# Gated cross-attention and mixture of experts: five more expert blocks with the weights as the stationary operand, and row scatters tied to VectorE's products

## The chip, the cores and the metric

The kernel runs on one core of one Trainium2 chip. The metric is device time in microseconds (us) of the whole program, the median of repeated executions of one compiled program. A separate execution was profiled; every duration quoted below comes from it.

## The reference, cut to what matters

32 sequences of 128 tokens with 128 features go through a cross-attention layer (16 heads, added through a tanh gate) and then through a layer of experts. The change lies in the expert layer alone:

```
h = layernorm(x)                                  # 4096 tokens x 128
scores = sigmoid(h @ gate_w.T)                    # 32 experts in 4 groups of 8
# the 2 best groups, in them the 8 best experts; weights normalised, times 2.5
final[t] = sum over the chosen e of w[t,e] * down_e( silu(h gate_e) * (h up_e) )
x = x + tanh(g_ffn) * (final + shared_mlp(h))
```

All data are float32. Every token uses the 16 experts of exactly two groups, those not chosen with weight zero. So a token is sorted by its pair of groups (six pairs), and a block is 128 tokens of one pair, which need two group halves of 8 experts with 64 hidden units each.

## The kernel before, in words

The program first does attention, 32 sequences one after another (up to about 300 us), then a stretch in which the last sequences, the shared expert and the sorting overlap (to about 334 us), then a loop over expert blocks, number j = 0 to 34, which the profile shows from 334 us to about 536 us. Two more blocks stand behind a branch at the end.

**Sorting in three batches.** `choose(k)` is a generator that does the expert choice and computes a row number for each token. It is advanced in small pieces by `gap(room, transfers)`, placed by hand into the instruction order; after its pieces `gap` issues up to `transfers` waiting scatters through `put_rows`. One scatter is `put(i)`, L698: GpSimd (POOL) writes 128 token rows (16 weights, 128 features, the token's number; 145 floats) to their sorted places in the DRAM table `xs`. The batches have 12, 8 and 12 scatters. Batch 2 serves the last stage, blocks 15 to 36; batch 1 serves blocks 7 to 14 and batch 0 blocks 0 to 6. `SHARE` is (7, 8, 22), `NBLK` is 37 and `NSURE` is 35.

**Loading.** `load(j)`, L1100, reads a block's 128 sorted rows into `xb` on the queue of SyncE (SP), in 16 buffers. The first load of a batch waits for all its scatters to land. `more_loads(must, may)` issues loads up to block `must` in any case, and up to `may` once the scatters of that batch have all been issued.

**Two forms of a block.** In a narrow block `xprep` turns the tokens on TensorE (PE, L1116), `gate_up` makes two products of 512 columns, the tokens being the stationary operand (L1124, L1126), VectorE (DVE) multiplies by weights (`uw`, L1131) and by the SiLU (`h`, L1136), and `turned_hidden` turns the hidden values on PE (L1144) and copies them out on ScalarE (ACT, L1146). In a wide block the expert weights are stationary: `gate_up_wide` makes 16 matmuls of 128 columns per half (L1190), the hidden values come out turned already, and no `turned_hidden` is needed. In exchange ACT copies the group's weights to a fixed place (`place_weights`, L1182, two copies per half), and the routing weights must stand as 128 equal rows: `turn_weights` transposes them on PE (L1158, L1159) and sends 8 KB to DRAM (`wr`, L1165, on SP), and `spread_weights` reads that back into `wb` with two broadcast transfers of 256 KB (L1170, on SP). DVE then uses `wb` (L1196) and makes `h` (L1198). Both forms end in `down` (L1206) and `finish`: ACT scales the result (`o`, L1215) and POOL adds it to the output rows with an indirect DMA (L1217).

**The order in the loop.** It is written out by hand. Iteration j issues the two halves of block j + 1's gate and up products, with block j's `down` between them, `xprep` or `place_weights` for j + 2, and at its end `turn_weights` and `spread_weights` for block j + 3 if that is wide. A block's token number column is read by DVE in `number` (L1112), which waits for the load. All engines run their own instructions in order. The products g and u have two PSUM buffers each.

```
    def wide(j):
        return j >= NBLK - SHARE[2] + 2      # 17 and above
```

Of the kernel before, what the change touches and what calls it, by code (L numbers as in the profile page):

```python
# [12 lines left out]
ALU = mybir.AluOpType  # L13
# [24 lines left out]
NBLK = B + NC - 1  # L38
TAIL = (NC - 1) * P
NSURE = NBLK - 2  # L40
# [8 lines left out]
SHARE = (FULL[0], FULL[1] - FULL[0], NBLK - FULL[1])  # L49
# [5 lines left out]
def gated_cross_attention_moe(  # L55
# [236 lines left out]
    v = nc.vector  # L292
# [213 lines left out]

    filled = {-1: base}
    sorts = []
    tab = const.tile([1, NBLK, 4], I32, tag="tab", name="tab")
    ready = [False] * 3  # L510

    def choose(k):
# [5 lines left out]
        def small(name, *shape):  # L518
            return r1.tile([P, *shape], F32, tag=name, name=f"{name}_{k}")


        other = nc.gpsimd if k == 0 else v
# [74 lines left out]
        at = 0  # L597
        for g in range(NG - 1):
            w = NG - 1 - g
# [79 lines left out]
        row = small("row", n, NC)  # L679
# [17 lines left out]
        def put(i):  # L697
            w = nc.gpsimd.indirect_dma_start(  # L698
                out=xs[:, :], out_offset=bass.IndirectOffsetOnAxis(ap=posi[:, i : i + 1], axis=0),
                in_=rows[:, first[k] + i, :], in_offset=None, bounds_check=NROWS - 1,  # L700
            )

            if sorts:
                tc.declare_no_dep(w.ins, group="sorts", reason="no two tokens have one row")
            tc.add_to_no_dep_group("sorts", w.ins)
            sorts.append(w.ins.name)
# [83 lines left out]
    def step_on(value=None):  # L790
        try:
            piece[:] = [batches[0].send(value)]
        except StopIteration:
            batches.popleft()
            piece.clear()

    def put_rows(n):
        for _ in range(min(n, len(pending))):
            _, put, i = pending.popleft()
            put(i)  # L800

    def gap(room, transfers=1):

        fresh = True
        while batches and 3 - len(batches) < opened:
            if not piece:
                step_on()
                continue
            w = piece[0]
            if w == "n":  # L810
                if not fresh:
                    break
                step_on()
            elif w in ("pe", "act"):
                break
            else:
                if room <= 0:
                    break
                room -= w
                step_on()  # L820
            fresh = False
        put_rows(transfers)
# [259 lines left out]
    xbs, wrows, wbs, wcs, own, xTs, groups, hs, hTs, ys, idx = ({} for _ in range(11))  # L1082

    def stage(j):
        return max(i for i in range(3) if sum(SHARE[:i]) <= j)
# [35 lines left out]
    def gate_up(j, s):  # L1121
        at = groups[j][s] * FG
        g = ps_g.tile([P, FG], F32, tag="g", name=f"g_{j}_{s}")
        nc.tensor.matmul(g, xTs[j], eg_all[:, bass.ds(at, FG)], start=True, stop=True)  # L1124
        u = ps_g.tile([P, FG], F32, tag="u", name=f"u_{j}_{s}")
        nc.tensor.matmul(u, xTs[j], eu_all[:, bass.ds(at, FG)], start=True, stop=True)  # L1126
        a = m3.tile([P, FG], F32, tag="act", name=f"act_{j}_{s}")
        nc.scalar.activation(a, g, AF.Silu)
        uw = m3.tile([P, FG], F32, tag="uw", name=f"uw_{j}_{s}")
        w = xbs[j][:, 0:NEP].rearrange("p (t s q) -> p s q t", t=2, s=2)[:, s]  # L1130
        v.tensor_tensor(  # L1131
            uw.rearrange("p (q t f) -> p q t f", t=2, f=64), u.rearrange("p (q t f) -> p q t f", t=2, f=64),
            w.unsqueeze(3).to_broadcast([P, GE // 2, 2, 64]), ALU.mult,
        )
        h = m4.tile([P, FG], F32, tag="h", name=f"h_{j}_{s}")
        v.tensor_tensor(h, a, uw, ALU.mult)  # L1136
        hs[j, s] = h

    def turned_hidden(j, s):
        h = hs.pop((j, s))  # L1140
        n = FG // P
        pt = small_psum(f"ph_{j}_{s}").rearrange("p (q n) -> p q n", n=P)
        for q in range(n):
            nc.tensor.transpose(pt[:, q, :], h[:, q * P : (q + 1) * P], ident)  # L1144
        hT = m3.tile([P, n, P], F32, tag=f"hT{s}", name=f"hT_{j}_{s}")
        nc.scalar.copy(hT, pt)  # L1146
        hTs[j, s] = hT
# [3 lines left out]


    def wide(j):
        return j >= NBLK - SHARE[2] + 2

    def turn_weights(j):
        pt = small_psum(f"px_{j}").rearrange("p (k n) -> p k n", n=P)
# [26 lines left out]
    def gate_up_wide(j, s):  # L1184
        n = FG // P
        g, u = (ps_g.tile([P, n, P], F32, tag=k, name=f"{k}_{j}_{s}") for k in "gu")
        w = wcs.pop((j, s))
        for k, pt in enumerate((g, u)):
            for q in range(n):
                nc.tensor.matmul(  # L1190
                    pt[:, q, :], w[:, k, q * P : (q + 1) * P], xTs[j], start=True, stop=True
                )
        a = m3.tile([P, n, P], F32, tag="act", name=f"act_{j}_{s}")
        nc.scalar.activation(a, g, AF.Silu)
        uw = m3.tile([P, n, P], F32, tag="uw", name=f"uw_{j}_{s}")
        v.tensor_tensor(uw, u, wbs[j][:, s], ALU.mult)  # L1196
        hTs[j, s] = m4.tile([P, n, P], F32, tag="h", name=f"h_{j}_{s}")
        v.tensor_tensor(hTs[j, s], a, uw, ALU.mult)  # L1198

    def down(j, s):  # L1200
        hT = hTs.pop((j, s))
# [35 lines left out]
    AHEAD = 3  # L1237
# [5 lines left out]
    def more_loads(must, may):  # L1243
        while loaded_[0] < NSURE and (
            loaded_[0] <= must or (loaded_[0] <= may and complete(stage(loaded_[0])))
        ):
            load(loaded_[0])
            loaded_[0] += 1

    with tc.manual_schedule():  # L1250
        more_loads(AHEAD, AHEAD)
        hsh = {}

        def up(t):
            g = ps_g.tile([P, TT], F32, tag="g", name=f"sg_{t}")
            u = ps_g.tile([P, TT], F32, tag="u", name=f"su_{t}")
            up_products(t, g, u)
            a = m3.tile([P, TT], F32, tag="act", name=f"sa_{t}")
            hsh[t] = m4.tile([P, TT], F32, tag="h", name=f"sh_{t}")
            gated(g, u, a, hsh[t])  # L1260

        def down_base(t):
            y = ps_y.tile([P, TB, D], F32, tag="y", name=f"sy_{t}")
            down_products(y, hsh.pop(t))
            base_out(t, y, m4.tile([P, TB, D], F32, tag="so", name=f"so_{t}"))

        up(4)
        up(5)
        gap(1.2, 2)
        down_base(4)  # L1270
        psum_place("prs_4")
        gap(1.2, 2)
        up(6)
        pt = small_psum("pt2")
        turn2(pt, 28, 4)
        turned2_out(pt, 28, 4)
        down_base(5)
        gap(1.2, 2)
        pl = small_psum("pl2")[:, 0 : 8 * E]
        logits(pl, 24, 8)  # L1280
        logits_out(pl, 24, 8)
        psum_place("prs_5")
        logits_done(24, 8)
        up(7)
        gap(1.2, 2)
        xprep(0)
        down_base(6)
        psum_place("prs_6")
        gap(1.2, 2)
        opened = 3  # L1290
        gate_up(0, 0)
        xprep(1)
        down_base(7)
        gate_up(0, 1)
        for j in range(AHEAD + 1):
            number(j)
        turned_hidden(0, 0)
        done = -1
        for j in range(NSURE):
            more = j + 1 < NSURE  # L1300
            more_loads(j + AHEAD, j + 13)
            if more:
                (gate_up_wide if wide(j + 1) else gate_up)(j + 1, 0)
            if j + 2 < NSURE and wide(j + 2):
                place_weights(j + 2, 0)
            if done < j - 1:
                finish(j - 1)
                if j - 1 + AHEAD < NSURE:
                    number(j - 1 + AHEAD)
            down(j, 0)  # L1310
            if not wide(j):
                turned_hidden(j, 1)
            if j + 2 < NSURE and not wide(j + 2):
                xprep(j + 2)
            psum_place(f"prb_{j}")
            gap(1.4, 2)
            if more:
                (gate_up_wide if wide(j + 1) else gate_up)(j + 1, 1)
            if j + 2 < NSURE and wide(j + 2):
                place_weights(j + 2, 1)  # L1320
            down(j, 1)
            if not wide(j) or not more:
                finish(j)
                done = j
                if AHEAD < j + AHEAD < NSURE:
                    number(j + AHEAD)
            if more and not wide(j + 1):
                turned_hidden(j + 1, 0)
            if j + AHEAD < NSURE and wide(j + AHEAD):
                turn_weights(j + AHEAD)  # L1330
                spread_weights(j + AHEAD)
            gap(1.4, 1)

# [68 lines left out]
```

## Time and profile before

| what | value |
|---|---|
| median of 3 runs | 548.38 us (547.67 to 548.81) |
| profiled execution, its own time | 551.0 us |
| its span in the profile | 549.2 us |
| granted TensorE clock in it | 0.984 of full |
| PE / DVE / ACT / POOL busy | 94% / 74% / 68% / 50% |
| expert blocks: narrow, wide | 17, 18 |
| scatters of rows (L698) | 32, mean 1.08 us on POOL |
| additions to the output (L1217) | 35, mean 1.58 us on POOL |

The profiled execution's time is 1.8 us above its span, which is what lies around the span, and 2.6 us above the median of the runs. "PE" is TensorE's matmuls and "PEld" its weight loads, which overlap them. In a row of the timeline the columns are start, duration, engine, line, operation, what is written and read, how often, and in brackets the idle time before it with what ended it. "SPq" is the SP queue: such a row is the issue of a transfer and not its duration.

### The profile page before, as it was taken

Reading aid. Unit: us, or ns where it says so; the run is one execution under the profiler, and the core shown is the slowest. Engines: PE = TensorE matmul, PEld = TensorE weight load, DVE = VectorE, ACT = ScalarE, POOL = GpSimd, SP = SyncE. Lnnn points to the kernel's source line nnn. Section 1 sums busy time; section 2 is a strip of 40 time slices with the busy share of each in tenths; the row PEclk is TensorE's granted clock in tenths of the full one; section 3 lists DMA queues with packets and bytes.
Section 4 is the critical chain, followed back from the end, with each engine's and each line's share of the span. In section 5 each row is a group of like instructions: output and inputs, shape, how many; then the busy total and the mean of one; then the engine's idle time right before and its main releaser. Section 6 shows DMA issues by size and latency. Waiting matters only on the chain.

```text
span 549.2 us, 15741 instructions
## 1 busy us (share of the span) xinstructions
PE 514.8 (94%) x5857; PEld 440.9 (80%) x5857; DVE 406.1 (74%) x920; ACT 374.5 (68%) x1407; POOL 276.8 (50%) x248
## 2 busy tenths in 40 slices
PE   5889999999999999998999789999999999999992
PEld 4777888988989988897876556666676799999992
DVE  3779999898898998998887588898644445555551
ACT  1688989989899888997883144444444677777760
POOL 5255557665675756874754641652672212232332
PEclk9899999999999999999999989999999999999997
DMA  8994440805304010000000232131123255453631
GB/s 237 236 331 144 129 174 3 300 4 175 127 20 152 3 42 1 2 2 3 2 2 26 77 94 63 35 72 15 38 49 82 56 118 122 95 131 89 128 88 15
DMA packets 49563, 47.81 MB, mean 87 GB/s; under 512 B 20752, under 2 KB 38848, under 8 KB 49104
## 3 DMA queue, kind: packets, MB, share of 16 engines
q1 hardware_dynamic: 43008, 41.71, 26.6%
q0 software_dynamic: 6192, 4.56, 5.7%
q8 instruction: 48, 0.79, 0.6%
q10 hardware_dynamic: 288, 0.52, 0.4%
q14 instruction: 27, 0.22, 0.2%
HBM read 25.44 MB, written 21.54 MB: 86 GB/s over the span
## 4 chain that ended last, share of the span: by engine, by line
PE 71%; DVE 20%; POOL 2%; ACT 2%; issue 1%; DMA 1%; another core or an unknown queue 1%; POOLq 0%; DVEq 0%
PE y L1206 11%; PE o_ps L436 8%; PE s_ps L369 8%; PE o_ps L415 7%; PE u L1190 6%; PE g L1190 6%; PE o_ps L328 6%; PE g L1124 6%; PE u L1126 5%; DVE nmax L376 5%; DVE eT L404 5%; PE ph L1144 3%; DVE xn L307 3%; DVE oT L424 1%; ACT e L389 1%
## 5 line engine op out<-in xcount | busy, mean ns | idle before, releaser
L389 ACT ACTIVATE e<-s_ps,nmax 128x128 f32<-128x128 f32 x512 | 181.6, 384 | 9.7 <-DVE nmax L376 8.3
L398 POOL TENSOR_TENSOR e<-e,rs 128x1024 f32<-128x1024 f32 x64 | 121.4, 1898 | 92.6 <-DVE rs L396 92.6
L1217 POOL DMA_INDIRECT out_dram<-o,idx x35 | 55.1, 1575 | 128.0 <-ACT o L1215 74.9
L389 ACT ACTIVATION_READ_ACCUMULATOR e<-s_ps,nmax 128x1 f32 x512 | 114.0, 223 | 0.0
L376 DVE TENSOR_REDUCE nmax<-s_ps 128x8 f32<-128x1024 f32 x64 | 77.0, 1202 | 11.7 <-PE s_ps L369 11.5
L404 DVE STREAM_TRANSPOSE eT<-e 128x1024 f32<-128x1024 f32 x64 | 78.7, 1229 | 0.9 <-POOL e L398 0.9
L369 PE MATMUL s_ps<-kvT_sb,qT 64*128 64x128 f32 x1024 | 76.0, 289 | 3.0 <-ACT e L389 1.9
L369 PEld LDWEIGHTS s_ps<-kvT_sb,qT 64*128 64x128 f32 x1024 | 63.7, 191 | 18.7 <-issue 11.1
L436 PE MATMUL o_ps<-c_sb,oT 128*128 128x128 f32 x512 | 65.4, 281 | 6.8 <-DVE oT L424 6.8
L436 PEld LDWEIGHTS o_ps<-c_sb,oT 128*128 128x128 f32 x512 | 59.7, 191 | 13.4 <-DVE oT L424 10.5
L415 PE MATMUL o_ps<-eT,kv 32*64 32x256 f32 x2048 | 66.0, 380 | 2.1 <-DVE c_sb L285 1.0
L328 PE MATMUL o_ps<-xnT,a_sb 128*128 128x128 f32 x480 | 59.9, 278 | 0.0
L1196 DVE TENSOR_TENSOR uw<-u,wb 128x512 f32<-128x512 f32 x36 | 24.9, 692 | 46.4 <-PE u L1190 41.5
L328 PEld LDWEIGHTS o_ps<-xnT,a_sb 128*128 128x128 f32 x480 | 56.7, 194 | 0.3 <-issue 0.2
L415 PEld LDWEIGHTS o_ps<-eT,kv 32*64 32x64 f32 x2048 | 49.4, 131 | 8.1 <-DVE c_sb L285 1.4
L1206 PEld LDWEIGHTS y<-ed_sb,hT 128*128 128x128 f32 x272 | 35.5, 191 | 16.0 <-issue 14.3
L698 POOL DMA_INDIRECT xs<-rows,posi x32 | 34.5, 1078 | 19.7 <-DVE nbi L727 11.0
L1131 DVE TENSOR_TENSOR uw<-u,xb 128x512 f32<-128x512 f32 x34 | 23.3, 686 | 24.2 <-PE u L1126 22.5
L1146 ACT COPY hT<-ph 128x512 f32<-128x512 f32 x34 | 19.9, 586 | 27.1 <-PE ph L1144 20.0
L1190 PE MATMUL g<-xT,wc 128*128 128x128 f32 x288 | 38.0, 275 | 0.0
L1190 PE MATMUL u<-xT,wc 128*128 128x128 f32 x288 | 38.0, 275 | 0.0
L1206 PE MATMUL y<-ed_sb,h 128*128 x288 | 37.8, 275 | 0.0
(203 smaller groups left out, 891.2 us busy)
## 6 DMA issues: line engine op xcount, KB each, us to landing
xs<-zero SPq DMA_DIRECT2D x8, 1740.0 KB, 12.2
wb<-wr SPq DMA_DIRECT2D x36, 256.0 KB, 4.0
kv<-in_kv_dram SPq DMA_DIRECT2D x32, 128.0 KB, 3.1
xb<-xs SPq DMA_DIRECT2D x35, 72.5 KB, 2.2
x_all<-in_x_dram SPq DMA_DIRECT2D x8, 256.0 KB
kvT_sb<-in_kvT_dram SPq DMA_DIRECT2D x6, 256.0 KB, 5.5
eg_sb<-in_exp_gT_dram SPq DMA_DIRECT2D x1, 1024.0 KB, 6.2
eu_sb<-in_exp_uT_dram SPq DMA_DIRECT2D x1, 1024.0 KB
```

What stands on the lines that cost most here:

```text
L328: nc.tensor.matmul(o_ps[1][:, p // HP, p % HP * P : (p % HP + 1) * P], a_sb[:, p].rearrange("d j k -> d (j k)"), x_, start=True, stop=True,)
L369: nc.tensor.matmul(s_ps[g][:, j, q, :], qT[b][r, g * HP + q, :], kvT_sb[r, b * P : (b + 1) * P], start=True, stop=True,)
L376: v.tensor_reduce(nmax[b, g], s_ps[g].rearrange("p j q k -> p (j q) k"), AX.X, ALU.max, negate=True)
L389: nc.scalar.activation(es[b][:, g, j, q, :], s_ps[g][:, j, q, :], AF.Exp, bias=n[:, c], accum_out=sums[b, g][:, c],)
L398: nc.gpsimd.tensor_tensor(e, e, rs.unsqueeze(2).to_broadcast([P, NP, P]), ALU.mult)
L404: v.transpose(eTs[b][:, g].rearrange("p j q n -> p (j q n)"), es[b][:, g].rearrange("p j q n -> p (j q n)"))
L415: nc.tensor.matmul(o_ps[a // 2][j * KV : (j + 1) * KV, a % 2, 0 : NP * Q].rearrange("k (g q n) -> k g q n", g=2, q=HP), kv_sb[b // TB][r, ...
L436: nc.tensor.matmul(o_ps[0][:, 0, 0:D], o[:, p].rearrange("k a n -> k (a n)"), c_sb[:, p, :], start=(p == 0), stop=(p == NP - 1),)
L698: w = nc.gpsimd.indirect_dma_start(out=xs[:, :], out_offset=bass.IndirectOffsetOnAxis(ap=posi[:, i : i + 1], axis=0), in_=rows[:, first[k] ...
L1190: nc.tensor.matmul(pt[:, q, :], w[:, k, q * P : (q + 1) * P], xTs[j], start=True, stop=True)
L1206: nc.tensor.matmul(ys[j], hT[:, q, :], ed_all[:, bass.ds(groups[j][s] * FG + q * D, D)], start=(s == 0 and q == 0), stop=(s == 1 and q == ...
L1217: w = nc.gpsimd.indirect_dma_start(out=out_rows, out_offset=bass.IndirectOffsetOnAxis(ap=idx.pop(j), axis=0), in_=o, in_offset=None, bound ...
```

## The change

`wide` becomes true for blocks 10 to 14 as well, so the narrow blocks are 0 to 9, 15 and 16, and the wide ones 10 to 14 and 17 to 34. Each `h` product that DVE makes is noted in `pace`, and every scatter issued after the first such product waits for the latest one issued before it. The scatters that a `gap` issues change from two in the middle and one at the end of an iteration to one in the middle and two at the end. `more_loads` asks for block j + 2 in place of j + 3 where block j + 3 is narrow.

```diff
@@ choose
+    pace = []
...
             w = nc.gpsimd.indirect_dma_start(
                 out=xs[:, :], out_offset=bass.IndirectOffsetOnAxis(ap=posi[:, i : i + 1], axis=0),
                 in_=rows[:, first[k] + i, :], in_offset=None, bounds_check=NROWS - 1,
             )
+            if pace:
+                tc.add_manual_dep(
+                    w.ins, pace[-1],
+                    mybir.DependencyInfo(mybir.DependencyClass.Sync, mybir.DependencyReason.DATA),
+                    reason="not all at once: transfers in a row hold the other engines up",
+                )
@@ gate_up
-        v.tensor_tensor(h, a, uw, ALU.mult)
+        w = v.tensor_tensor(h, a, uw, ALU.mult)
         hs[j, s] = h
+        pace.append(w.ins.name)
@@ wide
-        return j >= NBLK - SHARE[2] + 2
+        at = j - (NBLK - SHARE[2])
+        return -5 <= at < 0 or at >= 2
@@ gate_up_wide
-        v.tensor_tensor(hTs[j, s], a, uw, ALU.mult)
+        w = v.tensor_tensor(hTs[j, s], a, uw, ALU.mult)
+        pace.append(w.ins.name)
@@ the loop over blocks
-            more_loads(j + AHEAD, j + 13)
+            more_loads(j + AHEAD if j + AHEAD < NSURE and wide(j + AHEAD) else j + 2, j + 13)
...
             psum_place(f"prb_{j}")
-            gap(1.4, 2)
+            gap(1.4, 1)
...
-            gap(1.4, 1)
+            gap(1.4, 2)
```

## The prediction

> **What bounds the kernel now.** I read the page's busy shares and slices first, then PE's timeline in the block loop, then stretches of it with their granted clock, then the timelines of POOL and SP where batch 2 is scattered and loaded.
>
> ```profile
> PE 514.8 (94%) x5857; PEld 440.9 (80%) x5857; DVE 406.1 (74%) x920; ACT 374.5 (68%) x1407; POOL 276.8 (50%) x248
> ...
> PE   5889999999999999998999789999999999999992
> ...
> wb<-wr SPq DMA_DIRECT2D x36, 256.0 KB, 4.0
> ...
> wr<-wq SPq DMA_DIRECT2D x18, 8.0 KB, 1.4
> ```
>
> PE is full from slice 25 to the last but one, so a PE instruction saved in the block loop is time saved, and any wait of PE is time lost. Two iterations, one narrow and one wide, and two idle stretches ahead of the loop (columns: stretch, sum of busy time, PE busy, granted clock, DMA share, GB/s):
>
> ```profile
> 399.57:405.77 6.20, 6.20 (x35) 1.00 0.23 46
> 443.13:448.71 5.58, 5.58 (x53) 1.00 0.56 118
> ...
> 310.00:313.40 3.40, 1.36 (x4) 1.00 0.08 22
> 313.40:316.80 3.40, 3.40 (x5) 0.50 0.34 96
> ...
> 323.60:327.00 3.40, 1.69 (x5) 1.00 0.24 55
> 327.00:330.40 3.40, 3.40 (x11) 0.51 0.67 187
> ```
>
> A narrow block costs PE 6.20 us, a wide one 5.58. After a stretch in which PE was busy for 1.36 or 1.69 of 3.4 us, the clock is halved for the next 3.4 us. Idle times of 0.6 us in the loop did not do that. Now the rows that decide block 14:
>
> ```profile
> 394.98 1.16 PE L1206 MATMUL y<-ed_sb,hT 128*128 x8 [0.32 <-ACT hT L1146]
> ...
> 400.49 1.56 POOL L1217 DMA_INDIRECT out_dram<-o,idx  x1 [0.30 <-issue]
> ...
> 408.62 1.45 POOL L698 DMA_INDIRECT xs<-rows,posi  x1 [0.30 <-issue]
> ...
> 411.69 12.23 SPq L1100 DMA_DIRECT2D xb<-xs  x13
> ...
> 425.24 1.02 PE L1126 MATMUL u<-eu_sb,xT 128*128 x2
> ...
> 431.54 0.34 SPq L1165 DMA_DIRECT2D wr<-wq  x1
> 432.92 1.11 SPq L1170 DMA_DIRECT2D wb<-wr  x2
> ```
>
> The last scatter of batch 2 leaves POOL at 410.07; SP issues the first load of the last stage 1.6 us later, and then 13 in a row at 0.94 us each. A block's `wr` and `wb` go over the same queue, in order.
>
> **The change part by part.**
>
> *PE work of five blocks.* Removed per block: two groups of four transposes (L1144), 0.436 us each. Added: one more token transpose, 0.11, and 16 short matmuls in place of 4 long ones, 0.895 against 0.860 us for each of four products. That is -0.87 + 0.11 + 0.14 = -0.62 us, which is 6.20 less 5.58. Five blocks: **-3.1 us**.
>
> *The hold at 394 us.* Iteration 9 takes 6.79 us instead of 6.20: ACT gets `y` and `ph` late, amid three scatters in a row, and `down` waits for `hT`. With block 10 wide, `down(9, 0)` comes 0.2 us later after the start, and `turned_hidden(10, 0)` is gone. **-0.6 us.** If the hold returns this is 0.
>
> *ACT.* In iteration 8 it has two SiLU (0.60), two hT copies (0.59), four weight copies (0.615), `o` (0.37) and the two copies of `turn_weights` (0.25): 5.7 of 6.3 us. Each hT copy ends before its `down` by my count (the tighter one at 393.7 for 394.9). Cost 0, covered by that 1.2 us; without the cover it delays PE by the excess, at most about 0.6 us.
>
> *The new waits on POOL.* A scatter waits for an `h` product that DVE makes in its own half iteration; queued behind it on POOL are later scatters and `finish`, and behind the last scatter the loads on SP. In batch 2 POOL is behind DVE anyway: after `finish(9)` it has five scatters at 1.30 us apart, and the awaited h(11, 1) is ready at 405.2, when POOL reaches its scatter at 405.5. So the waits bind hardly at all, and groups of three in a row remain. Batch 1: its last scatter now stands behind `finish(3)` and starts at about 362.8 instead of 361.1, so the load of block 7 lands at 367.5 instead of 365.8. DVE's `number(7)` is at its turn at 367.42, and DVE is full there: h(7, 0) ends 0.2 us before PE needs it. **+0.1 us**, between 0 and 0.8.
>
> *SP, and block 14.* This is the large one. Blocks 10 to 13 send their `wr` and `wb` while SP has nothing else, and their weights land 6.9 us after the transposes, as block 17's do now (430.58 to 437.5), ahead of use. Block 14's are issued at the end of iteration 11. But at the start of iteration 11 batch 2's scatters are all issued, and `may` (j + 13 = 24) lets ten loads, blocks 15 to 24, go onto SP ahead of them. In step:
> - Iteration 7 starts at 379.09 as now. Iterations 7 to 13 then last 7.70 (7.48 now, and the two transposes of `turn_weights`, 0.22), 6.31 (6.20 less `xprep`'s 0.11, and 0.22), 6.02 (four products at 0.895, two `down` at 0.89, one group of transposes, 0.22), 5.58, 5.58 (the wide form), 5.37 (no `turn_weights`) and 5.48 us (`xprep` of block 15 again); iteration 14 starts at 421.13.
> - `o(9)` is ready at 399.47, `finish(9)` runs from 399.7 to 401.3, the five scatters follow, the last from 406.8 if each takes 1.0 us. Five of the 20 scatters in the loop take 1.4 to 1.5 now, so I put its end at 408.4 and the load of block 15 at 410.0.
> - Ten loads: the tenth 8.43 us after the first (411.69 to 420.12 now). Then `wr` +0.46, first `wb` +1.38, second +0.52, landing +3.95 (block 17: 433.44 to about 437.4): 424.75.
> - DVE's uw(14, 0) starts at 424.85 and takes 0.69. PE can do g(15, 0) in the meantime, but u(15, 0) needs the PSUM buffer that uw(14, 0) reads. It starts at about 425.6 where it could have started at 421.99.
>
> So PE waits **+3.6 us** (2.6 to 4.8: the faster scatters, or POOL 1.2 us later as with the hold of now). In other words u(15, 0) stands at 425.6, where it is now at 425.24: all that the wide blocks won is waited away. After that, everything finds its data: h(14, 0) is done before u(15, 0) is, and DVE catches up within one iteration.
>
> *The clock after that wait.* The trace has no wait of this length inside the loop. The Trainium skill ("TensorE: Matmul & The Clock Gate", section "HAM oscillation — how this bites in real kernels") says that gaps above about 3.4 us are the ones to avoid, and its section "What's actually happening" lets the clock drop after one idle window of about 3.4 us. By that rule a wait of 3.6 us is at the limit, most often split over two windows, and costs 0. By the rows above, half a stretch of idling is enough: 3.4 us at 0.50, which loses 1.7 us of PE work. I take the rows: **+1.7 us** (0, or 2.8 if two stretches are hit).
>
> Sum: -3.1 - 0.6 + 0.1 + 3.6 + 1.7 = **+1.7 us**, on a span of 549.2; the same difference holds for the median of the runs: 548.4 + 1.7, **550.1 us**. The 1.8 us around the span do not change.
>
> **The rivals.**
>
> *A, the loads do not stand in the way.* If `wb` of block 14 came in time (SP's loads quicker, or the scatters far earlier), the sum would be -3.1 - 0.6 + 0.1 = -3.6: **544.8 us**. For it: blocks 17 and later show that the round trip fits. Against it: ten loads at 0.94 us each would have to shrink by half; the wait would need to be under 1.5 us, hence `wb` 2 us earlier than in my count with the short scatters.
>
> *B, the wait without the clock.* PE waits 3.0 to 3.6 us but the clock stays: -3.6 + 3.3 = -0.3: **548.1 us**. For it: the skill's limit. Against it: two rows of this trace.
>
> *C, DVE's backlog.* The load of block 7 lands later than counted, DVE stops at `number(7)` with its sorting work behind it, and with 0.2 us of slack at blocks 7 PE waits. It decides from the point where the last scatter of batch 1 starts after 362.9; each microsecond later is one lost. A start at 364.5 gives +1.5 beside the rest: **551.6 us**. Against it: three `h` products that these scatters wait for are ready before POOL gets to them.
>
> *D, the spreading does nothing.* The order on POOL stays finish, scatter, scatter, scatter. This is inside my forecast; it takes the 0.6 back, 550.7 us.
>
> **How the numbers follow.** About 0.2% (1.1 us) is what a measurement of this kernel can tell from no change. Forecast, with D, 48%: 549.6 to 551.3. C or two halved stretches, 10%: up to 552.2. B, 28%: 547.4 to 549.0. A, 14%: 544.5 to 547.0. Slower by over 0.2% (above 549.5) holds the forecast and C, 0.57; B is within, with the thin ends of the others, 0.30; A is faster, 0.13. Range 547.6 to 552.0: it leaves out A and the end of C. The likeliest case's own range is 549.6 to 551.3.
>
> **What would show it.** In the changed profile: DVE's `uw<-u,wb` waiting once for the `wb<-wr` transfer, for about 7 us (SP ten loads ahead of one `wr`); PE idle for about 3.6 us ahead of one u product of the narrow form, near 422 us, and the clock at 0.5 for 3.4 us right after; five blocks of 5.4 to 5.6 us before; the block loop from there as long as now. A missing wait on `wb`, or PE full through 420 to 430 us, makes the forecast wrong towards A; a full clock towards B; PE idle near 378 us shows C.

## The result and the profile after

The changed kernel takes 554.03 us (median of 4 runs, 552.61 to 554.55) beside 548.48 us for the kernel before, measured with it: a ratio of 1.0099, 95% interval 1.0078 to 1.0121. In numbers, 5.5 us slower; 550.1 was predicted, with 552.0 as the upper end. The profiled execution of after took 552.61 us (span 550.8), the fastest of the four.

The page of after, its busy shares, the 40 slices of PE and of its granted clock, and the spreading of weights:

```profile
PE 512.7 (93%) x5942; PEld 448.1 (81%) x5942; DVE 406.0 (74%) x920; ACT 380.5 (69%) x1422; POOL 275.2 (50%) x248
...
PE   5899999999999999998999979999996999999992
...
PEclk9899999999999999999999979999999999999997
...
wb<-wr SPq DMA_DIRECT2D x46, 256.0 KB, 3.7
```

PE's slice 31 (413 to 427 us) has a 6 where the kernel before had a 9. The clock's 7 in slice 24 lies ahead of the loop; a drop of 3.4 us that falls on two slices, as in slices 31 and 32, leaves 9 in both, so this row does not show it. The timeline of PE in after shows what ended there (the bracket is the idle time ahead):

```profile
419.44 1.02 PE L1131 MATMUL g<-eg_sb,xT 128*128 x2
425.65 2.07 PE L1133 MATMUL u<-eu_sb,xT 128*128 x2 [5.19 <-DVE uw L1205]
```

This is u of block 15, which needs the PSUM buffer that block 14's `uw` reads. DVE in after, at that `uw`:

```profile
424.90 0.69 DVE L1205 TENSOR_TENSOR uw<-u,wb 128x512 f32<-128x512 f32 x1 [10.14 <-DMA wb<-wr]
```

And SP's queue in after, which carries `wr` and `wb`:

```profile
403.51 0.31 SPq L1174 DMA_DIRECT2D wr<-wq  x1
406.26 1.08 SPq L1179 DMA_DIRECT2D wb<-wr  x2
409.11 8.87 SPq L1107 DMA_DIRECT2D xb<-xs  x10
418.07 0.38 SPq L1174 DMA_DIRECT2D wr<-wq  x1
420.26 1.10 SPq L1179 DMA_DIRECT2D wb<-wr  x2
```

Ten loads stand between block 13's `wb` and block 14's `wr`. The stretches around the wait in after (stretch, sum of busy time, PE busy, granted clock, DMA share, GB/s):

```profile
418.50:422.00 3.50, 1.96 (x12) 1.00 0.35 78
422.00:425.40 3.40, 0.00 (x0) 1.00 0.96 195
425.40:428.80 3.40, 3.15 (x9) 0.50 0.02 4
428.80:432.20 3.40, 3.40 (x21) 1.00 0.02 5
```

Behind the wait PE has half its clock for 3.4 us. During the wait the DMA engines are busy at 0.96: they bring the `wb` that DVE, and through it PE, waits for.

Iteration by iteration (from the start of one `down` to the next but one, PE's timeline), in us:

| iteration | before | after | predicted |
|---|---|---|---|
| 7 | 7.48 | 7.70 | 7.70 |
| 8 | 6.69 | 6.38 | 6.31 |
| 9 | 6.31 | 6.02 | 6.02 |
| 10, 11 | 6.20, 6.20 | 5.58, 5.57 | 5.58, 5.58 |
| 12 | 6.21 | 5.36 | 5.37 |
| 13, with the wait and most of the drop | 6.20 | 11.77 | 5.48, and wait and drop |
| 14, with the rest of the drop | 6.42 | 6.60 | as before, and drop |

So PE's work was predicted to within 0.1 us an iteration, and all of the error lies in the wait and around it.

### The profile page after: what moved, and what is told of

The parts are those of the page before. It is cut to its first block, busy times and chain, and to the rows that moved or that the text cites. A ratio compares the mean times of both kernels' runs of the same rounds, so it can differ in the third digit from the quotient of the medians.

```text
span 550.8 us, 15971 instructions
## 1 busy us (share of the span) xinstructions
PE 512.7 (93%) x5942; PEld 448.1 (81%) x5942; DVE 406.0 (74%) x920; ACT 380.5 (69%) x1422; POOL 275.2 (50%) x248
## 4 chain that ended last, share of the span: by engine, by line
PE 71%; DVE 19%; ACT 3%; POOL 2%; DMA 2%; issue 1%; POOLq 0%; SPq 0%; DVEq 0%
PE y L1216 11%; PE o_ps L436 8%; PE s_ps L369 8%; PE g L1199 7%; PE u L1199 7%; PE o_ps L415 7%; PE o_ps L328 6%; DVE nmax L376 5%; DVE eT L404 4%; PE u L1133 4%; PE g L1131 4%; DVE xn L307 3%; PE ph L1152 2%; ACT e L389 2%; DVE oT L424 1%
## 5 line engine op out<-in xcount | busy, mean ns | idle before, releaser
L1205 DVE TENSOR_TENSOR uw<-u,wb 128x512 f32<-128x512 f32 x46 | 31.8, 691 | 67.6 <-PE u L1199 53.7
L1216 PE MATMUL y<-ed_sb,h 128*128 x368 | 49.0, 277 | 0.0
L1199 PE MATMUL u<-xT,wc 128*128 128x128 f32 x368 | 48.6, 275 | 0.0
L1199 PE MATMUL g<-xT,wc 128*128 128x128 f32 x368 | 48.6, 275 | 0.0
L1216 PEld LDWEIGHTS y<-ed_sb,h 128*128 128x128 f32 x368 | 45.6, 195 | 1.5 <-issue 1.0
L1203 ACT ACTIVATE act<-g 128x512 f32<-128x512 f32 x46 | 27.5, 597 | 27.0 <-PE g L1199 27.0
L1199 PEld LDWEIGHTS u<-xT,wc 128*128 128x128 f32 x368 | 44.8, 192 | 0.0
L1199 PEld LDWEIGHTS g<-xT,wc 128*128 128x128 f32 x368 | 44.7, 192 | 0.0
```

The source lines that it names most:

```text
L1199: nc.tensor.matmul(pt[:, q, :], w[:, k, q * P : (q + 1) * P], xTs[j], start=True, stop=True)
L1216: nc.tensor.matmul(ys[j], hT[:, q, :], ed_all[:, bass.ds(groups[j][s] * FG + q * D, D)], start=(s == 0 and q == 0), stop=(s == 1 and q == ...
```

## The experiments

Below, "the loop" is the time from the first `prb` (a product of the sorting, in the middle of iteration 1) to the end of the span, in a kernel's profile. It leaves out the stretch ahead of the loop, where profiles of one kernel differ by up to 4.6 us. "Ratio" is against the kernel before, measured beside it, with its interval.

### Both kernels again

> The kernel before, unchanged, for a second profile and for the granted clock of several runs. The first profiled execution took 551.0 us, 2.6 above its median, and had two halved stretches ahead of the block loop. If these come and go with the phase of the clock's window, this profile shows fewer or others, and the runs differ by about 1.7 us for each. If the profile itself costs the 2.6 us, it does so here again, and the loop is longer in it than in the other runs.

> The changed kernel, unchanged, for a second profile, since the first one is 1.4 us below the median of its runs. Theory W (the wait for block 14's spread weights, and the halved clock after it): again one wait of VectorE for wb of 8 to 11 us, one of TensorE of 4 to 6.5 us ahead of u of block 15, one halved stretch of 3.4 us behind it. Rival P (the scatters' waits delay something in each iteration): TensorE idle in several places of iterations 1 to 11. About 554 us either way.

before_again: 548.20 us, ratio 1.0009 (0.9998 to 1.002); loop 204.15 us. after_again: 553.84 us, 1.0117 (1.0079 to 1.0155); loop 209.82 us. The prediction's profile of before had a loop of 204.73: the 0.58 us more is the hold at 394 us, which before_again does not have (its iterations 8 and 9 take 6.20 each). Of the later profiles extra_wb_end has it again (loop 204.93). In after_again PE's row at u of block 15:

```profile
426.40 2.08 PE L1133 MATMUL u<-eu_sb,xT 128*128 x2 [6.13 <-DVE uw L1205]
```

And its stretches of PE from the middle of the wait on:

```profile
424.30:427.75 3.45, 1.35 (x2) 0.51 0.42 80
427.75:431.20 3.45, 3.45 (x12) 0.50 0.02 5
```

The wait is 6.13 us and two stretches are halved, the first while PE still waits for most of it. The loop is 5.67 us longer than before_again's, which is the measured difference.

### Who stands in the way: loads and block 14

loads_later (iteration 11 may not load the last stage):

```diff
-            more_loads(j + AHEAD if j + AHEAD < NSURE and wide(j + AHEAD) else j + 2, j + 13)
+            more_loads(j + AHEAD if j + AHEAD < NSURE and wide(j + AHEAD) else j + 2, j + (3 if j == 11 else 13))
```

> The changed kernel, but iteration 11 may not load ahead of block 14: the ten loads of the last stage go onto SP one iteration later, behind block 14's wr and wb. Theory W: the wait for wb, TensorE's 5.2 us and the halved stretch after it go; the loop is shorter than before's by 3.1 us, 3.7 with the hold at 394 us; 544.5 to 546 us beside 548.4. Rival P, or the wide form being slow at this place by itself: still 551 us or more.

546.45 us, ratio 0.9982 (0.9968 to 0.9996). The long wait and the halved clock are gone, and 7.4 us with them. What is late next is block 15's own load; PE in loads_later:

```profile
417.69 0.33 PE L1123 MATMUL px<-ident,xb 128*128 128x128 f32 x1 [1.77 <-DMA xb<-xs]
418.42 1.13 PE L1199 MATMUL g<-xT,wc 128*128 128x128 f32 x8 [0.40 <-ACT xT L1125]
```

two_first (iteration 11 loads blocks 15 and 16, then block 14's `wr` and `wb` go, then the rest):

```diff
-            more_loads(j + AHEAD if j + AHEAD < NSURE and wide(j + AHEAD) else j + 2, j + 13)
+            more_loads(j + AHEAD if j + AHEAD < NSURE and wide(j + AHEAD) else j + 2, j + (5 if j == 11 else 13))
```

> The changed kernel, but iteration 11 may load only the two blocks that are needed next, 15 and 16; block 14's wr and wb follow, then the other loads. Theory W: neither the wait for wb nor that for block 15's tokens is left, so the whole 3.1 us of the five blocks is won: 544.5 to 545.2 beside 547.8 to 548.4. Rival (the last scatter lands late because of block 13's transfers, and with it everything behind it): TensorE waits 0.5 to 2 us near blocks 14 and 15 in this version too; 545.5 to 547.

546.37 us, 0.9978 (0.996 to 0.9996). Only the order on one queue differs from after, and 7.5 us go. It is still above what was expected: PE stands for 0.12, 0.23 and 0.42 us between 407.0 and 408.6, ahead of all those loads, and the loop (202.48) is 0.7 us longer than narrow14's below, which has one wide block less. wide10_12 below shows more of that standstill.

narrow14 and wide10_12 (four and three added blocks):

```diff
-        return -5 <= at < 0 or at >= 2
+        return -5 <= at < -1 or at >= 2      # wide10_12: at < -2
```

> The changed kernel with blocks 10 to 13 wide and block 14 narrow; everything else stays, the ten loads in iteration 11 too. Theory W: no weights stand behind the loads, so no wait; four blocks at 0.62 give -2.5, with the hold -3.1; 545.2 to 546.2 us. Rival P: 551 us or more. Rival L (ten loads in a row hurt whatever comes then, as the transfers that collide): between the two, with TensorE idle near the loads.

> The changed kernel with blocks 10 to 12 wide, 13 and 14 narrow. It asks why the first load came 2.5 to 4.9 us after the last scatter left POOL, 1.6 to 1.8 in the kernel before. Theory T (the two 256 KB transfers of block 13's wb share the DMA engines with the last scatter): without them the distance is back to 1.6 to 2.0 us. Rival (the waits, or the add to the output right behind the last scatter): it stays at 2.5 or more. The time should be 3 x 0.62 = 1.9 us below before, 546.0.

narrow14: 545.26 us, 0.9955 (0.994 to 0.997); the loop is 201.77, 2.38 less than before_again's, and 4 x 0.62 is 2.5. Of PE's waits only the 0.57 us at about 380 us is left, which before has too. So block 14 alone costs all the loss. wide10_12: 547.78 us, 0.9988 (0.9965 to 1.0011). Three blocks' 1.9 us are nearly given back, for PE waits 1.50 us for the turned tokens of block 13 (PE, ACT, PE):

```profile
404.88 0.27 PE L1123 MATMUL px<-ident,xb 128*128 128x128 f32 x1
...
409.02 0.27 ACT L1125 COPY xT<-px 128x128 f32<-128x128 f32 x1 [4.26 <-PE y L1216]
...
409.33 1.12 PE L1131 MATMUL g<-eg_sb,xT 128*128 x2 [1.50 <-ACT xT L1125]
```

The product was done at 405.15, but the trace records its signal, with those of the four products that ended up to 407.83, only from 408.96 to 409.27, and ACT stood until then. two_first has the like at 408.56 to 408.81. What held the signals up the trace does not tell, so this run and two_first price the wide blocks only with that standstill in them.

### The new waits of the scatters

no_pace is after without the waits; pace_only is before with them, with the other split of scatters and the other `must`, and no block made wide.

```diff
-            if pace:                                   # no_pace
+            if False:
...
-        return -5 <= at < 0 or at >= 2                 # pace_only
+        return at >= 2
```

> The changed kernel without the scatters' waits for VectorE's products. My sum says that they hardly bind, so 553.5 to 554.2, no change. If the waits are what makes the last scatter late (in the changed profile POOL pauses 0.85 us ahead of the last but one), its loads and block 14's weights come up to 0.9 us earlier and the time falls by as much: 552.9. If the waits did what they are meant for, the time rises.

> The kernel before with the waits of the scatters and the one and two scatters per gap, and no block made wide. Theory (the waits bind hardly at all, and the one that moves the last scatter of batch 1 behind finish costs 0.1 us): 548.0 to 548.6, ratio 0.9995 to 1.001. Rival (spreading frees ScalarE and so PE): 547 to 547.8. Rival (the later last scatter makes VectorE stop at block 7's number): 548.8 to 549.5, with a wait of PE near the seventh block.

no_pace: 554.12 us, 1.0139 (1.0078 to 1.0201), a wide interval; pace_only is the sharper of the two. pace_only: 548.03 us, 0.9999 (0.9986 to 1.0013), loop 204.15 as before_again's. The spreading neither helps nor harms; rival D was right on that.

### What the halved clock costs

filler, filler_short and filler_mid let PE multiply while it waits: matmuls of block 15's tokens with the identity into an unused part of PSUM, ahead of u.

```diff
+        if (j, s) == (15, 0):                      # the lines that place `spare` are left out
+            for _ in range(FILL):                      # 46, 21, 28
+                nc.tensor.matmul(spare[0], xTs[j], ident, start=True, stop=True)
```

> The changed kernel with 46 extra matmuls on TensorE right ahead of u of block 15, into a part of a PSUM bank that nobody reads; their results are not used. At 0.112 us they fill 5.2 us, about the wait. It separates the halved clock from the wait. Theory W with the clock: the wait for VectorE shrinks to under 1.5 us, the clock stays full after it, and the kernel is 1.7 to 2.6 us faster than the changed one, 551.2 to 552.2. Rival (the skill's limit of a whole idle window holds, and what followed the wait was something else): no change, 553.8.

> As filler, with 21 idle-filling matmuls in place of 46 (their results are not used). In filler each of the 46 took 0.227 us (10.43 us in all), not the 0.11 that I had counted, so PE was still at them 3.3 us after u of block 15 could have started. 21 of them last 4.8 us and end before the wait for wb does. Theory (the wait is as long as in after, and the halved clock behind it is a price of its own): PE stays at 1.00 behind the wait, u of block 15 starts as far behind the loop's start as in after, and the time is 1.7 to 2.4 us under after's 553.8: 551.4 to 552.2. Rival (the clock's drop is not a cost, for the work behind it has slack): 553.3 to 554.3. If PE's idle rest of 1 to 2 us halves the clock all the same, the time is that of after and nothing is told.

> As filler, with 28 matmuls (6.4 us at 0.227): filler's 46 ended 3.3 us after u of block 15 could have started, and filler_short's 21 left PE idle for 2.04 us, behind which its profile shows the halved clock again. The gap to be filled is 6.9 us from PE's last product to u. Theory (the halved clock is a price of its own, 1.7 to 2.4 us): idle rest about 0.5 us, clock 1.00 behind it, time 551.4 to 552.2 where after has 553.8 to 554.0. Rival (it costs nothing): 553.3 to 554.3, with a full clock.

filler: 555.54 us, 1.0155 (1.0096 to 1.0214), slower and not faster as expected, since a filling matmul takes 0.227 us and not 0.11, and PE was still filling 3.3 us after u could have started. Less that it would be 552.2, an estimate. filler_short: 552.34 us, 1.0093 (1.0059 to 1.0127), but the profile has the drop all the same, after 2.04 us of waiting:

```profile
422.30:424.32 2.02, 0.00 (x0) 1.00 0.41 89
424.32:425.30 0.98, 0.98 (x3) 1.00 0.28 12
425.30:428.70 3.40, 3.40 (x12) 0.50 0.15 16
```

So it says nothing of the clock. filler_mid: 551.71 us, 1.0064 (1.0046 to 1.0081), and its stretches stay at full clock:

```profile
418.00:425.20 7.20, 6.79 (x58) 1.00 0.45 104
425.20:428.60 3.40, 3.38 (x15) 1.00 0.21 19
```

By the medians filler_mid is 2.1 us under after_again. A measure that leaves out the length of the wait is the time from the start of u of block 15 to the end of the span. It is 123.55 (filler) and 123.74 (filler_mid) at full clock, and 123.54 to 123.55 in loads_later, two_first and wide8_two, which have no long wait; 125.18 (after), 125.26 (no_pace), 125.74 (filler_short) and 125.97 (after_again) with the drop. The halved clock costs 1.4 to 2.4 us.

### Why the wait was longer than counted

In after, SP issues the first load 2.47 us after the last scatter left POOL (after_again 3.91), not 1.6. SP waits there for the scatter's signals that its rows have landed. From the scatter's start on POOL to the landing (us, the last number) in before_again, after and after_again, in this order:

```profile
xs<-rows,posi POOLq DMA_INDIRECT x1, 2.5
...
xs<-rows,posi POOLq DMA_INDIRECT x1, 3.1
...
xs<-rows,posi POOLq DMA_INDIRECT x1, 4.6
```

Over the runs this goes with block 13's `wb`. extra_wb and extra_wb_end put such a pair of transfers into the kernel before; nobody reads them.

```diff
             psum_place(f"prb_{j}")
+            if j == 10:                                # extra_wb
+                turn_weights(13)
+                spread_weights(13)
...
-            if j + AHEAD < NSURE and wide(j + AHEAD):
+            if j + AHEAD < NSURE and (wide(j + AHEAD) or j == 10):   # extra_wb_end
```

> The kernel before, in which block 13, still narrow, has its routing weights turned and spread all the same, in the middle of iteration 10; nobody reads them. So a pair of wb transfers (512 KB) is on its way when the last scatter of batch 2 leaves POOL. Theory (a wb pair issued ahead of the last scatter holds up the scatter's packets): the first load of block 15 is issued 2.5 to 5 us after the last scatter left POOL, where it is 1.62 and 1.79 in the two profiles of before. Rival (what comes late in after is due to the wide blocks' other work or to the waits): below 2 us. The time itself hardly moves, 0 to +0.5 us.

> As extra_wb, with the turning and spreading of block 13 (again read by nobody) half an iteration later, at the end of iteration 10. In extra_wb the pair of wb transfers was issued 4.3 us before the last scatter left POOL (402.94 against 407.28), its packets were through at 407.0, the scatter's own ran from 407.5 to 408.2, and the first load came 1.63 us behind the scatter: the two had not met. Here the pair should be issued at about 406, some 1.3 us ahead of the scatter's end. Theory (packets of wb ahead of the scatter's packets hold them up): first load 2.4 to 5 us after the scatter left POOL. Rival (the late loads of after have another cause): below 2 us.

extra_wb (548.72 us, 1.0011, 0.9999 to 1.0023) came too early: its pair was issued 4.3 us before the scatter left POOL and was through, and the load came 1.63 us after. extra_wb_end (550.65 us where before had 551.16, 1.0001, 0.9977 to 1.0026) met it. POOL in extra_wb_end, the last scatter:

```profile
407.57 1.02 POOL L698 DMA_INDIRECT xs<-rows,posi  x1 [0.31 <-issue]
```

SP in extra_wb_end:

```profile
407.14 1.11 SPq L1170 DMA_DIRECT2D wb<-wr  x2
412.84 9.49 SPq L1100 DMA_DIRECT2D xb<-xs  x10
```

The first load is issued 4.25 us after the scatter left POOL (407.57 + 1.02). pace_only has nothing on SP there; its last scatter on POOL and first load on SP:

```profile
406.32 0.99 POOL L699 DMA_INDIRECT xs<-rows,posi  x1 [0.30 <-issue]
```

```profile
408.95 3.02 SPq L1107 DMA_DIRECT2D xb<-xs  x4
```

That is 1.64 us. The runs, by when the pair of `wb` was issued; "landed" is the last of the scatter's signals among the trace's semaphore records, or the end of SP's wait for them where some are missing (wide10_12, extra_wb_end, filler). Both times count from the scatter's end on POOL:

| pair issued, from the last scatter's end on POOL | landed, us | first load, us |
|---|---|---|
| none near (before, before_again, pace_only), or 4.3 us ahead (extra_wb) | 1.34, 1.51, 1.36, 1.35 | 1.62, 1.79, 1.64, 1.63 |
| 5.8 us ahead (wide10_12) | 1.55 | 2.33 |
| 0.66 to 1.44 us ahead (two_first, after_again, narrow14, no_pace, extra_wb_end) | 3.49, 3.58, 4.55, 4.71, 3.74 | 3.81, 3.91, 4.88, 5.04, 4.25 |
| 0.12 to 0.58 us ahead (filler_mid, after, filler) | 2.00, 2.14, 2.04 | 2.33, 2.47, 2.41 |
| 0.22 to 0.42 us behind (filler_short, wide8_13, wide8_two) | 1.64, 1.38, 1.57 | 2.06, 2.15, 2.27 |

So the landing is late only where the pair goes out 0.1 to 1.4 us ahead of the scatter's end. In the last row it is the queue that is late: SP issues the pair until 1.3 to 1.5 us, and the load 0.76 us behind that. In wide10_12 SP passes its wait at 1.55 us and then stands 0.58 us, in the standstill told above.

That a pair of `wb` under way holds up the landing is shown by extra_wb_end, which adds only that (and the transposes and copies for it). An addition to the output, which many of these runs have on POOL right behind the scatter, is not needed for it: in extra_wb_end it comes 2.97 us later. The packets in the trace say where the time goes. In after_again the scatter's rows are written 1.70 to 2.54 us after its end on POOL, among the packets of `wb` (0.54 to 4.83); in before at 0.59 to 0.93. In after they are written on time (0.58 to 0.93) and only the signals come late, beside `wb` (from 0.86). What makes the packets and the signals wait stays open.

### More wide blocks

wide8_13 is narrow14 with blocks 8 and 9 wide as well; wide8_two is two_first with them.

```diff
-        return -5 <= at < 0 or at >= 2
+        return -7 <= at < -1 or at >= 2      # wide8_two: at < 0, and the loads of two_first
```

> As narrow14, with blocks 8 and 9 wide as well: six blocks added, none behind the ten loads. Theory (each wide block gives its 0.62 us as long as its wb lands in time): 548.2 - 6 x 0.62 = 544.5, which is 1.2 under what four blocks give; PE without a wait over 0.6 us in the loop. Rival (VectorE's sorting of batch 2 and the copies of ScalarE leave no room for the wide form in iterations 5 to 8): PE waits there, and the two blocks give nothing or lose: 545.3 to 547.

> As two_first (blocks 15 and 16 alone are loaded ahead of block 14's wr and wb), with blocks 8 and 9 wide as well: seven blocks added. Theory (only the order on SP's queue made the long wait): no wait over 1 us, 548.2 - 7 x 0.62 = 543.9, if the small waits of two_first stay 545.1. Rival (block 14 costs more in waits than its 0.62 us wherever its wr stands): above wide8_13 by 0.5 us or more.

wide8_13: 544.21 us, 0.993 (0.9901 to 0.9959), loop 199.58. wide8_two: 542.08 us, **0.9892 (0.9859 to 0.9924)**, loop 198.95: 6.0 us faster than before by the medians (548.04 beside it), and 12 faster than after (9 to 11 by the loops). The loop is 5.2 us shorter than before_again's: 7 x 0.62 is 4.3, and a wait of 0.57 us of PE in iteration 7, which all the other kernels have at about 380 us, is gone in both of these. Its loop is also 0.63 us shorter than wide8_13's, so block 14 now gives its 0.62, in one profile of each. SP's queue in wide8_two:

```profile
404.35 1.09 SPq L1179 DMA_DIRECT2D wb<-wr  x2
406.19 1.35 SPq L1107 DMA_DIRECT2D xb<-xs  x2
407.59 0.43 SPq L1174 DMA_DIRECT2D wr<-wq  x1
410.32 1.09 SPq L1179 DMA_DIRECT2D wb<-wr  x2
411.94 9.88 SPq L1107 DMA_DIRECT2D xb<-xs  x11
```

Block 14's `wb` is issued at 410.32, behind two loads, where after has it behind ten. The page of wide8_two:

```profile
PE   5889999999999999998999979999999999999992
...
PEclk9899999999999999999999999999999999999998
```

Slice 31 is full again.

## Why the prediction was right or wrong

Right: the sign, the place and the chain. Block 14's `wr` behind ten loads, `uw` waiting for `wb` (10.14 us in after, where about 7 was expected; two more waits of 1.8 and 2.0 us did not reach PE), u of block 15 waiting for `uw`, the halved clock behind. two_first and narrow14 show that this is all of the loss.

- *PE work of five blocks, -3.1*: right. The iterations agree, and four blocks give 2.38 us in narrow14.
- *The hold at 394 us, -0.6*: wrong as a gain over the median. It was in the profile that the sum was made on (loop 204.73) and later in extra_wb_end, and not in before_again or pace_only (204.15 both). Against those this term is 0. A stall that some executions have was counted as the kernel's.
- *ACT, 0, and the load of block 7, +0.1*: nothing against them; iterations 3 to 6 take 6.20 to 6.28 us in after, 6.20 to 6.21 in before, so rival C did not happen.
- *The waits on POOL*: right, they bind hardly at all (pace_only 0.9999).
- *PE waits for block 14's `wb`, +3.6 (2.6 to 4.8)*: **the step that failed**, in its size and not in its chain. It measured 5.19, 6.13 and 6.35 us (after, after_again, no_pace). In after, on the times of its own loop (its first `prb` stands 1.75 us earlier than in the profile before), the first load comes at 409.11 and not at 408.25, +0.86: the landing beside block 13's `wb`. From there to `wr` it is 8.96 us against 8.89. From `wr` to `wb` it is 2.19 us and not 1.38, +0.81. The two carry the 1.6 us that are missing. In after_again and no_pace the landing alone gives most of it: their first loads come 3.91 and 5.04 us behind the scatter, and their `wr` to `wb` takes 1.67 and 1.69. I took both terms from rows where the queue and the DMA engines were quiet (blocks 15 and 17 before), although the sum itself put a `wb` and ten loads there. What stretches `wr` to `wb` was not isolated: in wide8_13 it takes 2.8 to 4.6 us for blocks 9 to 13, with no loads ahead of it.
- *The end of the last scatter*, part of the same sum: 406.64 against 408.4 - 1.75 = 406.65, and that is luck. The scatters took 1.0 us each and not the longer times for which 0.6 us had been allowed, while POOL stood 0.85 us in place of 0.30 ahead of the last but one, for which nothing had been.
- *The clock, +1.7 (0 or 2.8)*: right. It is 1.4 to 2.4 us by the time from u to the end. Rival B, which rested on the Trainium skill's one idle window of about 3.4 us ("TensorE: Matmul & The Clock Gate", section "What's actually happening"), is out: the clock dropped in after, after_again and no_pace. Waits of over 5 us would let it drop by that rule too. But in no_pace it dropped 2.83 us into the wait (at 421.60, the wait begins at 418.77), and in filler_short 2.04 us of idling sufficed: the measurement decides, and 3.4 us is too long a limit.
- *The sum*: with measured terms, after_again's is -3.1 + 0 + 6.1 + 2.4 = +5.4 us (the 2.4 being half of the 4.8 us that PE worked at half clock, 1.35 + 3.45), and 553.84 - 548.20 is 5.6. The upper end of the range took either a longer wait or a second halved stretch; with both (4.8 and 2.8) and no hold, its own bounds give -3.1 + 0.1 + 4.8 + 2.8 = +4.6, or 553.0.

## What to carry to other kernels

A queue that runs in order is a resource like an engine: before a small transfer that something waits for is put on it, ask which burst can be issued just ahead of it, and let through only those loads of the burst that are needed first. Price each transfer in a new place with the load that the change itself puts around it, not from its quiet row: there the round trip of 8 KB took 1.4 us, behind ten loads 1.7 to 3.8. And a term of the sum that rests on one stall in one profile needs a second profile.

## What the runs showed of the hardware

- A scatter of 128 rows has landed 1.3 to 1.5 us after it leaves POOL when the DMA engines are free of other work, and 3.5 to 4.7 us when 512 KB of broadcast reads were issued 0.7 to 1.4 us before its end; the load that waits for it goes out at 1.6 to 1.8 and at 3.8 to 5.0 us.
- The halved clock in all profiles from 300 us to the end of the loop: every wait of PE of 2.39 us and more was followed by it. Of four waits of 1.99 to 2.04 us two were (at 312.0 in before, at 424.3 in filler_short) and two were not (both in extra_wb_end). Ten waits of 1.12 to 1.86 us were not, and one of 1.21 us, in before, was. So the length of the wait alone does not decide it.
- The drop lasted 3.4 or 6.8 us there, whatever the wait's length between 1.2 and 6.4 us.
- The signals that PE's products are done can come late: in wide10_12 those of five products that ended from 405.05 to 407.83 are recorded from 408.96 to 409.27. Why stays open.
